# Layer 2's experts on two rows at a time, a channel mix step behind its load, and shorter routing, in a four-layer fp32 forward pass

## The chip, the core and the metric

The kernel runs on one core of a Trainium2 chip. The core has a matmul engine (PE, whose weight loads are listed as PEld), a vector engine (DVE), a scalar engine (ACT), GpSimd (POOL) and SyncE (SP), which here only issues DMA transfers. Every engine works through its own queue in order. All of them read and write the on-chip SBUF; PE writes its results to PSUM. The metric is the device time of the program in microseconds (us), measured on the slowest core, of which there is one.

## What is computed

The input x has 4 rows (the batch) of 512 tokens with 128 features, in fp32. Each of the four layers does the same three things: half a feed-forward block, an attention block, half a feed-forward block, each on a layernorm of x and added to x.

```python
x = x + 0.5 * ffn_i(layernorm(x))
x = x + attn_i(layernorm(x))
x = x + 0.5 * ffn_i(layernorm(x))
```

Layer 0 has a mixture of 8 experts (top 2) and attention with 16 heads of 64; layer 1 a low-rank mixture and a windowed attention; layers 2 and 3 attention with 16 heads of 8, causal in layer 2. The change lies mostly in layer 2's feed-forward block. It is a switch with capacity, row by row:

```python
gates = softmax(tokens @ Wg)                     # 8 experts
expert = argmax(gates)                           # one expert a token
pos = running count of the tokens of that expert in this row
keep = pos < 64                                  # 512 tokens / 8 experts
h = gelu(kept tokens of expert e @ W1[e])        # 128 -> 512
output = gate * (h @ W2[e])                      # 512 -> 128; 0 for tokens not kept
```

Layer 3's feed-forward block is a channel mix: each token is blended with the one before it, by mu and 1 - mu, ahead of its projections.

## The kernel before, in words

Up to about 600 us the program does layer 0's first experts and its attention, and this part is the same in both versions. From there on (line 2636 and below) everything else is one pool of generator "processes": `tile0` to `tile19` (layer 0's second mixture, two blocks of 128 sorted tokens each, `tiled`, L848), `first0` to `first3` (all of layer 1 for one row), and, for n = 0 to 7, which are the four rows ahead of layer 2's attention and the same four behind it, `send{n}`, `take{n}` and `mix{n}`. The attentions of layers 2 and 3 are eight rows k = 0 to 7 (`begin{k}`, then the common processes `turning`, `scoring`, `weighing`, `masking`, `values`, then `turned` and `end{k}`), and layer 3's channel mix is `channels0` to `channels6`.

A process yields requests: an engine (or several that could do the step), a duration, the buffers it needs, and events that it waits for. A loop (`run`, L1413) keeps a clock of its own for each engine, picks the request that can start first, breaks near ties by a rank (`RANK`, L52, a table of tuned numbers), and lets the process issue its instructions. So the order of the instructions on every engine is fixed when the program is built, by these written durations, ranks and surcharges (`DEARER`). On the chip every engine keeps that order, whatever the true durations are.

The steps that the change touches:

- `l2_sent` (L2270, process `send`): layernorm, transposes to features by tokens (L1512), logits (L2283), then the routing on DVE, with an exp on ACT (L2289) in its middle, the running count as two matmuls (L2169, L2170), more DVE, and four indirect DMAs by GpSimd (L2327) that scatter the tokens into slots of a DRAM buffer `row_x`, 64 slots for each expert.
- `l2_taken` (L2335, process `take`): SP loads the row's sorted slots as X (L2345); four transposes (L2351); 32 up matmuls (L2366) with a 128x128 piece of W1 as weights and 64 slots moving; copies out of PSUM; four GELUs on ACT (L2376), which load their function table first; 32 down matmuls (L2384) with 64 columns of hidden units as weights, two side by side in the array; copies; a store to `row_y` (L2393).
- `l2_added` (L2396, process `mix`): four indirect gathers (L2409) and four adds into x (L2415).
- `to_heads` (L2660, process `heads`): once all tiles are done, their pools are released, and SP issues the loads of W2 and of both attentions' and the channel mix's weights, 23 DMAs (L2511). Then `l3_others` (L2418) puts one small DVE step (`nmu` = 1 - mu, L2420) into DVE's order. `heads_at_once` (L1831) writes ones into two V buffers with GpSimd.
- In the heads' attention `scoring` (L1931) and `values` (L1973) are PE's part and the exp (L1947) ACT's. A step covers four heads and one block of 128 keys.

`take{n}` follows `take{n-1}` or `take{n-2}`, `mix{n}` follows `take{n}`, and attention row k begins after `mix{k}` (layer 2) or after the channel mix (layer 3).

Of the kernel before, what the change touches and what calls it, by code (L numbers as in the profile page):

```python
# [11 lines left out]
F32 = mybir.dt.float32  # L12
AF = mybir.ActivationFunctionType
# [4 lines left out]
P = 128  # L18
# [22 lines left out]
def done(b):  # L41
# [9 lines left out]
CLOSE = 0.05  # L51
RANK = {  # L52
    "begin0": 7.13, "begin1": 16.87, "begin2": 2.08, "begin3": -4, "begin4": 2.25, "begin5": 16.3, "begin6": 18.65, "begin7": 5.19,
    "channels0": 2.52, "channels1": 8.5, "channels2": 0.21, "channels3": -14.23, "channels4": 27.64, "channels5": 35.57, "channels6": 55.73,
    "end0": -14.5, "end1": 16.73, "end2": 9.28, "end3": -13.76, "end4": 20.26, "end5": 8.69, "end6": 7.09, "fetching": 36.35, "first0": 12.23,
    "first1": 12.99, "first2": 13.46, "first3": 15.39, "half0": -16.36, "half1": -8.54, "kept0": 9.26, "looked": 68.09, "looked0": 55.15,
    "looked1": 38.53, "looked2": 55.16, "looked3": 44.23, "looked4": 53.01, "looked5": 64.26, "looked6": 56.59, "masking": 45.18, "mix0": 9.64,
    "mix1": 11.51, "mix2": 7.93, "mix3": -7.76, "mix4": 13.42, "mix5": 20.24, "mix6": 9.63, "mix7": 16.21, "placing": -4.73, "scoring": 23.21,
    "send0": -6.03, "send1": 10.23, "send2": 15.94, "send3": 6.71, "send4": 33.89, "send5": 9.79, "send6": 16.23, "send7": 37.79, "take0": -3.51,
    "take1": -6.11, "take2": 22.65, "take3": 5.52, "take4": 16.36, "take5": 23.51, "take6": 10.29, "take7": 21.36, "tile0": 8.75, "tile1": 6.94,  # L60
    "tile2": 4.64, "tile3": 9.21, "tile4": 1.92, "tile5": 9.1, "tile6": -2.3, "tile7": 4.99, "tile8": 9.81, "tile9": 10.06, "tile10": 10.38,
    "tile11": 10.39, "tile12": 11.4, "tile13": 11.41, "tile14": 11.42, "tile15": 10.69, "tile16": 12.44, "tile17": 12.45, "tile18": 12.46,
    "tile19": 12.87, "turning": 58.41, "values": 43.5, "weighing": 38.58, "whole_l2": 4.79, "whole_l3": 12.44,
}
FETCH = 4.0
DEARER = {"PE": 0.0, "ACT": 0, "DVE": 0.3, "POOL": 0.5, "SP": 0.0}
END = object()

def shape_constants():
    c = {}
# [195 lines left out]
def program(ctx: ExitStack, tc: tile.TileContext, a: dict, out: bass.AP, worst):  # L268
# [1562 lines left out]
    def heads_at_once(procs, rows, w, work, w3, late):  # L1831
# [5 lines left out]
        for t in V:  # L1837
            nc.gpsimd.memset(t, 1.0)
# [891 lines left out]
```

## Time and profile before

| | us |
|---|---|
| median of 3 runs (lowest, highest) | 1293.74 (1288.74, 1293.77) |
| the profiled execution's own time | 1290.51 |
| its span, from the first to the last instruction | 1288.7 |
| PE busy | 1158.0 |
| DVE busy | 891.8 |
| ACT busy | 707.1 |
| GpSimd busy | 341.4 |
| mean granted PE clock, share of full speed | 0.958 |

The span is one execution, and the page's durations come from it. PE busy sums intervals whose ends are modelled, since matmuls are pipelined. A row of the groups names line, engine, operation, output and inputs, shapes and count, then busy time, mean of one instruction and the idle time of the engine just ahead of it, with the work that ended it. A row of the timeline begins with start and length in us. Matmuls in fp32 leave two records each, transposes one.

### The profile page before, as it was taken

To read this page: it belongs to the slowest core of one execution; us is meant where nothing else is said; L and a number is where in the kernel's file an instruction comes from. 1 tells how busy PE (TensorE), PEld (TensorE's weight loads), DVE (VectorE), ACT (ScalarE), POOL (GpSimd) and SP (SyncE) were. 2 spreads that over 40 slices of the span, in tenths; PEclk is the share of its full clock that TensorE was granted. 3 is DMA by queue.
4 is the path that set the end of the run, shared out by engine and by line. 5 is a ranking of instruction groups with operands and counts; after the bars stand their busy time and mean duration, and the time that the engine had idled before them with its cause. 6 is when DMAs were issued, how large, how long until landed. Compare 5 with 4: busy or idle time off the path is not lost.

```text
span 1288.7 us, 20383 instructions
## 1 busy us (share of the span) xinstructions
PE 1158.0 (90%) x7066; PEld 614.1 (48%) x7066; DVE 891.8 (69%) x2342; ACT 707.1 (55%) x1030; POOL 341.4 (26%) x323
## 2 busy tenths in 40 slices
PE   5899989999989999997998848798998999999994
PEld 3455544334425335364555426474675665443332
DVE  5697777988988998769668737876637655344233
ACT  2435545654644635442444424466777778778882
POOL 4430223022310400202134535623325233111010
PEclk9899989999999999998999958898999999999998
DMA  8123312111111111101321130001100010000000
GB/s 308 35 72 90 89 57 68 66 60 40 60 62 50 66 50 49 51 1 48 117 66 48 34 109 25 20 16 34 35 25 27 16 34 18 17 25 2 9 9 11
DMA packets 63490, 65.02 MB, mean 50 GB/s; under 512 B 11538, under 2 KB 53907, under 8 KB 62867
## 3 DMA queue, kind: packets, MB, share of 16 engines
q1 hardware_dynamic: 57236, 51.04, 11.8%
q0 software_dynamic: 6144, 12.60, 3.3%
q8 instruction: 59, 0.97, 0.3%
q14 instruction: 51, 0.42, 0.1%
HBM read 29.13 MB, written 17.69 MB: 36 GB/s over the span
## 4 chain that ended last, share of the span: by engine, by line
PE 62%; DVE 18%; issue 8%; DMA 4%; POOL 3%; ACT 3%; SPq 1%; POOLq 0%; DVEq 0%; ACTq 0%
PE big L1931 8%; PE one L1973 7%; PE big L1200 6%; PE one L1214 6%; PE one L2366 4%; PE big L880 3%; PE big L758 3%; PE one L1243 2%; PE one L1522 2%; PE big L603 2%; DMA yg<-sorted_y,ito 2%; DVE sums L1209 2%; PE one L2384 2%; PE big L1150 1%; PE one L1994 1%
## 5 line engine op out<-in xcount | busy, mean ns | idle before, releaser
L1947 ACT ACTIVATE pT<-big 128x1024 f32<-128x1024 f32 (+1 forms) x224 | 205.9, 964 | 43.5 <-PE big L1931 36.7
L1201 ACT ACTIVATE pT<-big 128x1024 f32<-128x1024 f32 x128 | 125.7, 1034 | 54.9 <-PE big L1200 52.8
L1200 PE MATMUL big<-qk 64*128 64x512 f32 x512 | 126.6, 605 | 6.8 <-DVE U L1236 6.8
L1931 PE MATMUL big<-qkq,qkk 32*128 32x512 f32 (+3 forms) x1024 | 127.3, 553 | 1.2 <-ACT pT L1947 1.0
L1214 PE MATMUL one<-pT,V 128*64 128x512 f32 x512 | 116.9, 598 | 0.0
L1973 PE MATMUL one<-pT,V 128*32 128x512 f32 (+3 forms) x1024 | 112.1, 526 | 0.9 <-DVE own L1537 0.6
L583 POOL DMA_INDIRECT sorted_x<-xn,irows x64 | 72.5, 1133 | 69.6 <-DVE share L555 22.4
L1485 POOL TENSOR_TENSOR rs<-rs,root 128x4 f32<-128x4 f32 x35 | 37.4, 1068 | 170.3 <-DVE rs L1483 116.0
L1209 DVE TENSOR_TENSOR sums<-sums,pT 128x1024 f32<-128x1024 f32 x64 | 78.1, 1220 | 5.1 <-ACT qk L1152 0.5
L1200 PEld LDWEIGHTS big<-qk 64*128 64x128 f32 x512 | 46.3, 186 | 69.0 <-issue 40.3
L880 PE MATMUL big<-w_w,xsT 128*128 x156 | 75.3, 614 | 1.8 <-ACT xsT L1352 1.2
L1931 PEld LDWEIGHTS big<-qkq,qkk 32*128 32x128 f32 x1024 | 46.6, 183 | 58.7 <-issue 39.5
L758 PE MATMUL big<-w_w,xsT 128*128 x156 | 73.5, 594 | 0.3 <-issue 0.3
L1291 ACT COPY U<-one 128x512 f32<-128x512 f32 x32 | 18.8, 587 | 94.9 <-PE one L1214 92.8
L839 POOL DMA_INDIRECT yg<-sorted_y,ito x32 | 38.4, 1200 | 122.4 <-DMA sorted_y<-ys 61.5
L1214 PEld LDWEIGHTS one<-pT,V 128*64 128x64 f32 x512 | 33.9, 136 | 77.1 <-issue 72.4
L603 PE MATMUL big<-xnT,w_w 128*128 128x512 f32 x128 | 61.2, 614 | 6.9 <-DVE u L608 5.8
L1959 DVE TENSOR_TENSOR pT<-pT,w_c_tri 128x256 f32<-128x256 f32 (+1 forms) x96 | 48.1, 524 | 21.0 <-ACT pT L1947 20.7
L2366 PEld LDWEIGHTS one<-XT,w_l_w 128*128 128x128 f32 x464 | 54.1, 192 | 12.4 <-ACT hr L1352 4.8
L2366 PE MATMUL one<-XT,w_l_w 128*128 128x64 f32 x464 | 57.2, 276 | 0.7 <-DVE x L350 0.3
L2409 POOL DMA_INDIRECT yg<-row_y,islot x32 | 34.2, 1070 | 75.5 <-DMA row_y<-y 67.9
L605 ACT ACTIVATE t<-big,w_bs 128x512 f32<-128x512 f32 x32 | 21.7, 685 | 56.0 <-PE big L603 33.7
(435 smaller groups left out, 2333.6 us busy)
## 6 DMA issues: line engine op xcount, KB each, us to landing
other<-qk SPq DMA_DIRECT2D x64, 256.0 KB, 2.3
xs<-sorted_x SPq DMA_DIRECT2D x78, 64.0 KB, 1.8
sorted_y<-ys SPq DMA_DIRECT2D x38, 128.0 KB, 1.8
w_w<-in_w SPq DMA_DIRECT2D x2, 2048.0 KB, 13.6
w_l_w<-in_l_w SPq DMA_DIRECT2D x8, 256.0 KB, 3.0
w_l_w<-in_l_w SPq DMA_DIRECT2D x1, 2048.0 KB, 7.7
X<-row_x SPq DMA_DIRECT2D x8, 256.0 KB, 2.8
row_y<-y SPq DMA_DIRECT2D x8, 256.0 KB, 2.3
```

The lines of the kernel that those rows point to most:

```text
L583: apart(nc.gpsimd.indirect_dma_start(out=sorted_x[:, :], out_offset=bass.IndirectOffsetOnAxis(ap=irows[:, b, j, t : t + 1], axis=0), in_=x ...
L603: nc.tensor.matmul(pa[:, m, :], lhsT=w["w13"][:, NE, m, odd, c * P : (c + 1) * P], rhs=xTs[b], start=True, stop=True)
L758: nc.tensor.matmul(pa[:, k, :], lhsT=st[u]["xT"][:, k * P : (k + 1) * P], rhs=w["w13"][:, bass.ds(st[u]["e"][k], 1), m].rearrange("p o a b ...
L880: nc.tensor.matmul(pa[:, k, :], lhsT=xT[:, k * P : (k + 1) * P], rhs=w["w13"][:, bass.ds(e[k], 1), m].rearrange("p o a b -> p (o a b)"), s ...
L1200: nc.tensor.matmul(sT[:, u, :], lhsT=k[r, t * P : (t + 1) * P], rhs=q[r, :], start=True, stop=True)
L1201: nc.scalar.activation(pT[:, :, t % 2, :], sT, AF.Exp, scale=scale)
L1209: nc.vector.tensor_tensor(s, s, pT[:, :, m, :], ALU.add)
L1214: nc.tensor.matmul(po[r, :], lhsT=V[:, t, :], rhs=pT[:, u, t % 2, :], start=(t == 0), stop=(t == NT - 1), tile_position=(0, 64 * u))
L1931: nc.tensor.matmul(sT[j // 2][:, j % 2, c : c + n], lhsT=keys[k][r, t * P : (t + 1) * P], rhs=turns[k, g][r, S - n :], start=True, stop=True)
L1947: nc.scalar.activation(p[:, :, :n], sets[i][h][:, :, :n], AF.Exp, scale=scale)
L1973: nc.tensor.matmul(po[32 * j : 32 * j + 32, S - n :], lhsT=V[k % 2][:, t, NJ * g + j, :], rhs=us[i][j // 2][:, j % 2, c : c + n], start=(t ...
L2366: nc.tensor.matmul(ph[:, j, c, :], lhsT=w["l2_w1"][:, 2 * q + j, c * P : (c + 1) * P], rhs=XT[:, 2 * q + j, :], start=True, stop=True)
```

## The change

1. Layer 2's experts on two rows. `PAIRS = (2, 4, 6)`: rows 0 and 1 keep `l2_taken`; rows 2 and 3, 4 and 5, 6 and 7 go through the new `l2_taken2`, which waits for both sends, loads both rows' X, and lays the transposes side by side, so that an up matmul moves 128 columns (64 slots of each row) against a piece of W1, and a down matmul has 128 columns of hidden units as weights. It stores each row's half of y apart. `mix` of the first row of a pair waits for the common take.
2. The channel mix step `nmu` becomes a process of its own, `others`, that waits for the event `loaded_l3`; `channels0` to `channels3` wait for it. The two memsets of V become processes too (`ones0`, `ones1`).
3. Shorter routing: the gate is 1 / (2 x the sum of exps), so the shares are not formed; the first maximum is found by comparing the logits less their maximum with 0; the exp is off the way to the slots. 21 DVE instructions behind the row's maximum become 18.
4. New durations in many requests, a new rank table, and other surcharges; `turning` no longer offers GpSimd. A helper `kept_warm` is added, whose loop runs over an empty tuple.

The diff, without the rank table and most of the changed durations:

```diff
 }
+PAIRS = (2, 4, 6)
 FETCH = 4.0
-DEARER = {"PE": 0.0, "ACT": 0, "DVE": 0.3, "POOL": 0.5, "SP": 0.0}
+DEARER2 = {"PE": 0.0, "ACT": 0, "DVE": 0.3, "POOL": 0.2, "SP": 0.0}
+DEARER = {"PE": 0.0, "ACT": 0.1, "DVE": 0.3, "POOL": 0.2, "SP": 0.0}
...
+    def kept_warm(t):
+
+        for kind, n, make in () and (("big", 3, big), ("one", 2, one)):
+            a = when(kind, n)
...
                 if t is not None:
-                    e = min(r.ways, key=lambda e: max(t, busy_till[e]) + r.ways[e] + DEARER[e])
+                    dearer = DEARER2 if "begin0" in events else DEARER
+                    e = min(r.ways, key=lambda e: max(t, busy_till[e]) + r.ways[e] + dearer[e])
...
             us = p.req.ways[e]
+            if e == "PE":
+                kept_warm(t)
...
         V = [work.tile([P, NT, H, 32], F32, tag=f"V{m}", name=f"V{m}") for m in range(2)]
-        for t in V:
-            nc.gpsimd.memset(t, 1.0)
         queries, keys, turns, inverse, through = {}, {}, {}, {}, {}
+
+        def ones_in(m):
+            yield POOL(1.9)
+            nc.gpsimd.memset(V[m], 1.0)
+
+        for m in range(2):
+            clock.procs.append(process(f"ones{m}", ones_in(m), 12.0 + 20 * m))
+            clock.procs[-1].ready = clock.done
...
             tokens(pv, xnT, w[layer + "_wv"])
-            yield moving(S, wait=[f"valued{k - 2}"] if k > 1 else [])
+            yield moving(S, wait=[f"valued{k - 2}"] if k > 1 else [f"ones{k}"])
             moved(V[k % 2][:, :, :, :DH].rearrange("p t h d -> p (t h) d"), pv.rearrange("p (n d) -> p n d", d=DH))
...
                 for g in range(NG):
-                    yield any_of({"DVE": 0.46, "ACT": 0.6, "POOL": 0.8}, "qkq", wait=f"q{k}", at=0.0)
+                    yield any_of({"DVE": 0.49, "ACT": 0.72}, "qkq", wait=f"q{k}", at=0.0)
...
 
         return [route(i, b) for i, b in enumerate(rows)], rest()
 
-    def l2_mixed(w, work, b, rooms, key, late):
+    def l2_mixed(w, work, b, rooms, key, late, single):
 
         sent, kept = [], []
-        return l2_sent(w, work, b, rooms, key, sent, kept), l2_taken(w, work, b, rooms, sent, late), l2_added(work, b, rooms, kept, late)
+        take = l2_taken(w, work, b, rooms, sent, late) if single else None
+        return l2_sent(w, work, b, rooms, key, sent, kept), take, l2_added(work, b, rooms, kept, late), sent
 
     def l2_sent(w, work, b, rooms, key, sent, kept):
 
...
+        t0 = clock.done
+        m, order, ex = little([P, NT, NE], "chosen"), little([P, NT, NE], "order"), little([P, NT, NE], "exs")
         gate, best = little([P, NT], "gates"), little([P, NT], "best")
         sofar = little([P, NT - 1, NE], "sofar")
-        yield DVE(1.0)
-        nc.vector.tensor_reduce(sm, sh, AX.X, ALU.add)
-        nc.vector.reciprocal(sm, sm)
-        nc.vector.tensor_tensor(sh, sh, wide(sm, NT), ALU.mult)
-        nc.vector.tensor_reduce(best, sh, AX.X, ALU.max)
-        nc.vector.tensor_scalar(gate, best, 0.5, None, ALU.mult)
-        yield DVE(1.4)
-        nc.vector.tensor_tensor(order, sh, wide(best, NT), ALU.is_equal)
-        nc.vector.tensor_tensor(order, order, w["c_first"].unsqueeze(1).to_broadcast([P, NT, NE]), ALU.mult)
+        yield DVE(1.1)
+        nc.vector.scalar_tensor_tensor(order, sh, 0.0, w["c_first"].unsqueeze(1).to_broadcast([P, NT, NE]), ALU.is_equal, ALU.mult)
         nc.vector.tensor_reduce(best, order, AX.X, ALU.max)
         nc.vector.tensor_tensor(m, order, wide(best, NT), ALU.is_equal)
         nc.vector.tensor_copy(sofar[:, 0, :], m[:, 0, :])
         for t in range(1, NT - 1):
             nc.vector.tensor_tensor(sofar[:, t, :], sofar[:, t - 1, :], m[:, t, :], ALU.add)
-        yield PE(0.5, "psum")
+        t1 = clock.done
+        yield ACT(0.24, at=t0)
+        nc.scalar.activation(ex, sh, AF.Exp)
+        t2 = clock.done
+        yield PE(0.55, "psum", at=t1)
         pp, k = spare()
         before = pp[:, : NT * NE].rearrange("p (t e) -> p t e", t=NT)
         l2_counts(before, m, sofar, w)
+        t3 = clock.done
         islot = little([P, NT], "islot", mybir.dt.int32)
         at, place, slot = little([P, NT, NE], "at"), little([P, NT], "place"), little([P, NT], "slot")
         kept += [gate, islot]
-        yield DVE(1.4)
+        yield DVE(0.85, at=max(t1, t2))
+        nc.vector.tensor_tensor(at, m, w["c_slot0"].unsqueeze(1).to_broadcast([P, NT, NE]), ALU.mult)
+        nc.vector.tensor_reduce(slot, at, AX.X, ALU.add)
+        nc.vector.tensor_reduce(sm, ex, AX.X, ALU.add)
+        nc.vector.tensor_scalar(sm, sm, 2.0, None, ALU.mult)
+        nc.vector.reciprocal(gate, sm)
+        yield DVE(1.15, at=max(clock.done, t3))
         nc.vector.tensor_tensor(order, before, m, ALU.mult)
         free(k)
         nc.vector.tensor_reduce(place, order, AX.X, ALU.add)
-        nc.vector.tensor_tensor(at, m, w["c_slot0"].unsqueeze(1).to_broadcast([P, NT, NE]), ALU.mult)
-        nc.vector.tensor_reduce(slot, at, AX.X, ALU.add)
         nc.vector.tensor_tensor(slot, slot, place, ALU.add)
         nc.vector.tensor_scalar(place, place, float(CAP), float(4 * none), ALU.is_ge, ALU.mult)
         nc.vector.tensor_tensor(slot, slot, place, ALU.add)
...
-            h = work.tile([P, 2, NH, CAP], F32, tag="hr", name="hr", bufs=n * NE // 2)
+            h = work.tile([P, 2, NH, CAP], F32, tag="hr", name="hr", bufs=NE if late else NE // 2)
             moved(h, ph)
             free(k)
             hs.append(h)
         free(kx)
-        yield ACT(2.6 + 2.6)
+        yield ACT(4.8)
         for h in hs:
             nc.scalar.activation(h, h, AF.Gelu_apprx_tanh)
         t0 = clock.done
...
         nc.sync.dma_start(out=ys[:none, :].rearrange("(q p) d -> p q d", p=P), in_=y)
         free(kx, clock.done + 2.5)
+
+    def l2_taken2(w, get, both):
+
+        work = get()
+        NH = HID // P
+        none = NE * CAP
+        X, landed = [], []
+        for rooms, sent in both:
+            yield ask("SP", 0.05, "Xl")
+            took("Xl")
+            X.append(work.tile([P, NT, D], F32, tag="X", name="X", bufs=2))
+            ld = nc.sync.dma_start(out=X[-1], in_=rooms[0][:none, :].rearrange("(q p) d -> p q d", p=P)).ins
+            for k in sent:
+                tc.add_manual_dep(ld, k.name, mybir.DependencyInfo(mybir.DependencyClass.Sync, mybir.DependencyReason.DATA), reason="all tokens' slots")
+            landed.append(clock.done + 5.0)
+        XT = None
+        for i in range(2):
+            yield PE(0.62, "psum", at=landed[i])
+            pt, k = spare()
+            for j in range(4):
+                nc.tensor.transpose(pt[:, j * P : (j + 1) * P], X[i][:, j, :], ident)
+            free("Xl")
+            yield moving(S, *(["wide"] if i == 0 else []))
+            if i == 0:
+                took("wide")
+                XT = work.tile([P, NE, 2, CAP], F32, tag="wide", name="XT", bufs=2)
+            moved(XT[:, :, i, :], pt.rearrange("p (e c) -> p e c", e=NE))
+            free(k)
+        t0 = clock.done
+        hs = []
+        for e in range(NE):
+            yield PE(0.96, "psum", at=t0)
+            ph, k = spare()
+            for c in range(NH):
+                nc.tensor.matmul(ph[:, c * P : (c + 1) * P], lhsT=w["l2_w1"][:, e, c * P : (c + 1) * P], rhs=XT[:, e].rearrange("p i c -> p (i c)"), start=True, stop=True)
+            yield moving(S, "hl")
+            took("hl")
+            h = work.tile([P, NH, P], F32, tag="hr", name="hr", bufs=NE)
+            moved(h.rearrange("p c m -> p (c m)"), ph)
+            free(k)
+            hs.append(h)
+        free("wide")
+        gone, y = [], None
+        for q in range(2):
+            yield ACT(4.8)
+            for h in hs[4 * q : 4 * q + 4]:
+                nc.scalar.activation(h, h, AF.Gelu_apprx_tanh)
+            gone.append(clock.done)
+        for q in range(2):
+            yield PE(3.7, "psum", at=gone[q])
+            py, k = spare()
+            for e in range(4):
+                for c in range(NH):
+                    nc.tensor.matmul(py[:, e * D : (e + 1) * D], lhsT=hs[4 * q + e][:, c, :], rhs=w["l2_w2"][:, 4 * q + e, c, :], start=(c == 0), stop=(c == NH - 1))
+            for _ in range(4):
+                free("hl")
+            yield moving(S, *(["wide"] if q == 0 else []))
+            if q == 0:
+                took("wide")
+                y = work.tile([P, NE, D], F32, tag="wide", name="y", bufs=2)
+            moved(y[:, 4 * q : 4 * q + 4, :].rearrange("p e d -> p (e d)"), py)
+            free(k)
+        for i, (rooms, _) in enumerate(both):
+            nc.sync.dma_start(out=rooms[1][:none, :].rearrange("(e c) d -> c e d", c=CAP), in_=y[CAP * i : CAP * i + CAP])
+        free("wide", clock.done + 2.5)
 
     def l2_added(get, b, rooms, kept, late):
 
...
     qkv = [None] * B
     for kind, n in (("one", 2), ("big", 3), ("xns", 3), ("sT", 4), ("pr", 5), ("pv", 1), ("yb", 5)):
         room(kind, n)
-    for kind, n in (("xn", 3), ("X", 2), ("h", 4), ("yg", 4), ("Xl", 4), ("hl", 8), ("ygl", 4), ("cx", 2), ("t0", 1), ("t1", 1), ("kT3", 1), ("r3", 1)):
+    for kind, n in (("xn", 3), ("X", 2), ("h", 4), ("yg", 4), ("Xl", 2), ("wide", 2), ("hl", 8), ("ygl", 4), ("cx", 2), ("t0", 1), ("t1", 1), ("kT3", 1), ("r3", 1)):
         room(kind, n)
     procs, pools, idle = [], [], [lambda: True]
     rows = [(n, b, causal) for n, causal in (("l2", True), ("l3", False)) for b in range(B)]
...
         yield ask("SP", 0.1)
         right[3].release()
         pools.append(pool("late", side="right"))
+
+    def others(w3):
+        yield DVE(0.2)
+        l3_others(w3, pools[0])
 
     def to_heads():
         yield ask("SP", 0.1)
...
         w2.update(loads(pools[-1], ["l2_w2"], later=behind))
         wa, w3 = heads_weights(pools[-1], behind)
         brought(behind)
-        l3_others(w3, pools[-1])
         events["second"], events["loaded_l2"], events["loaded_l3"] = (clock.done + t for t in (15.0, 22.0, 26.0))
         work = pool("work")
         pools.append(work)
-        yield POOL(3.7)
+        procs.append(process("others", others(w3), 9.0, ["loaded_l3"]))
         idle[0] = heads_at_once(procs, rows, wa, work, w3, late)
         for b in range(B):
-            procs.append(process(f"channels{b}", l3_ffn(b, w3, late, False), 10 + B + b, [f"mix{B + b}", "change"]))
+            procs.append(process(f"channels{b}", l3_ffn(b, w3, late, False), 10 + B + b, [f"mix{B + b}", "change", "others"]))
         for b in range(B - 1):
             procs.append(process(f"channels{B + b}", l3_ffn(b, w3, late, True), 40, [f"end{B + b}"]))
 
...
         clock.done += 4.0
 
     def mixture(n, b, after):
-        first = n < B
-        send, take, add = l2_mixed(w2, (lambda: pools[1]) if first else late, b, row_rooms[b], f"slots{n}", not first)
+        single = n not in PAIRS and n - 1 not in PAIRS
+        send, take, add, sent[n] = l2_mixed(w2, (lambda: pools[1]) if n < B else late, b, row_rooms[b], f"slots{n}", n >= B, single)
         procs.append(process(f"send{n}", send, 10 + n, [after]))
-        k = n - 1 if first else n - 2
-        procs.append(process(f"take{n}", take, 10 + n, [f"send{n}", "fetching", "heads"] + ([f"take{k}"] if k >= 0 else []) + ([] if first else ["change"])))
-        procs.append(process(f"mix{n}", add, 10 + n, [f"take{n}"] + ([f"mix{n - 1}"] if n else [])))
-
-    for b in range(B):
-        mixture(b, b, f"first{b}")
-        mixture(B + b, b, f"end{b}")
+        if single:
+            procs.append(process(f"take{n}", take, 10 + n, [f"send{n}", "fetching", "heads" if n < B else "change"] + ([f"take{n - 1}"] if n else [])))
+        elif n - 1 in PAIRS:
+            pair = [(row_rooms[m % B], sent[m]) for m in (n - 1, n)]
+            procs.append(process(f"take{n}", l2_taken2(w2, late, pair), 10 + n, [f"send{n - 1}", f"send{n}", "fetching", "change"] + ([f"take{n - 2}"] if n > 1 else [])))
+        procs.append(process(f"mix{n}", add, 10 + n, [f"take{n if single or n - 1 in PAIRS else n + 1}"] + ([f"mix{n - 1}"] if n else [])))
+
+    sent = {}
+    for n in range(2 * B):
+        mixture(n, n % B, f"first{n}" if n < B else f"end{n - B}")
 
     units = mix2.tiled(tiles, iwho)
     procs += units
```

## Prediction

> **What bounds the kernel now.** I read the page's sums and slices first, then busy time by stage, then the order of time around the one stage that is not full, and last the groups that the change rewrites.
>
> ```profile
> PE 1158.0 (90%) x7066; PEld 614.1 (48%) x7066; DVE 891.8 (69%) x2342; ACT 707.1 (55%) x1030; POOL 341.4 (26%) x323
> PE   5899989999989999997998848798998999999994
> PEclk9899989999999999998999958898999999999998
> ```
>
> TensorE is busy nine tenths of the span and no other engine seven. One slice, around 750 us, is at 4, and the granted clock falls to 5 with it. By stage (columns: window, length, then busy us and count of PE, PEld, DVE, ACT, POOL, then clock):
>
> ```profile
> 680.00:740.00 60.00, 51.28 (x227) 30.93 (x226) 50.06 (x145) 30.09 (x61) 30.62 (x29) 0.95 0.14 39
> 740.00:775.00 35.00, 17.73 (x52) 11.67 (x52) 13.04 (x64) 8.11 (x21) 13.61 (x13) 0.55 0.33 103
> 775.00:850.00 75.00, 58.93 (x398) 42.92 (x397) 62.97 (x218) 35.30 (x73) 41.53 (x37) 0.89 0.08 24
> 850.00:900.00 50.00, 44.23 (x424) 29.51 (x424) 31.26 (x122) 31.27 (x51) 14.24 (x13) 0.93 0.08 22
> 900.00:1000.00 100.00, 96.14 (x998) 65.07 (x998) 61.54 (x215) 74.94 (x111) 35.83 (x32) 1.00 0.10 29
> 1000.00:1100.00 100.00, 98.49 (x905) 57.34 (x901) 60.27 (x210) 76.76 (x111) 32.50 (x29) 1.00 0.08 24
> 1100.00:1180.00 80.00, 79.88 (x616) 37.17 (x620) 35.18 (x109) 62.62 (x79) 10.93 (x10) 1.00 0.05 14
> ```
>
> From 900 to 1180 us PE is without gaps while ACT, the next, idles a quarter of the time: there a microsecond of matmul taken away is a microsecond of span. From 740 to 900 PE idles 17.3 + 16.1 + 5.8 = 39 us: there the chains bind. The timeline tells the first hole:
>
> ```profile
> ...
> 754.45 0.43 SPq L2511 DMA_DIRECT2D w_l_mu<-in_l_mu  x1
> ...
> 755.87 0.43 SPq L2511 DMA_DIRECT2D w_l3f_wv<-in_l3f_wv  x1
> ...
> 757.42 0.17 DVE L2420 TENSOR_SCALAR nmu<-w_l_mu 128x2 f32<-128x2 f32 x1 [16.77 <-DMA w_l_mu<-in_l_mu]
> ...
> 758.93 2.07 PE L1522 MATMUL one<-w_lora_up,dT 128*128 128x128 f32 x8 [14.71 <-ACT dT L1364]
> ```
>
> At 741.58 us SP began the 23 loads of the heads' weights. VectorE came at once to the small step on l3_mu, the 20th of them, and stood 16.8 us; everything behind it on DVE stood too, and PE idled 14.7 us. What the change rewrites, as groups (busy us, mean ns of one, idle before):
>
> ```profile
> L2366 PE MATMUL one<-XT,w_l_w 128*128 128x64 f32 x464 | 57.2, 276 | 0.7 <-DVE x L350 0.3 <-ACT hr L1352 0.2
> ...
> L2384 PE MATMUL one<-w_l_w,hr 128*64 128x128 f32 x448 | 27.5, 276 | 0.1
> ...
> L2376 ACT ACT_TABLE_LOAD x8 | 10.3, 1283 | 0.1
> ```
>
> and one stretch of the chain in order of time (start, us, what):
>
> ```profile
> 303.52 7.34 PE one L1243 x64
> ```
>
> An up matmul (L2366: 64 columns move against 128x128 weights) costs 57.2/464 = 0.123 us. L1243, in the chain, moves 128 columns with new weights each time at 7.34/64 = 0.115: twice the columns cost no more. A down matmul (L2384, two 64-column tiles side by side) costs 27.5/448 = 0.061. An fp32 matmul leaves two records.
>
> **The change, part by part. A: experts on two rows.** For the six rows 2 to 7, 6 x 64 = 384 up records go, 384 x 0.123 = 47.2 us; 192 of 128 columns come, at 0.115 to 0.123: 22 to 23.6. The 384 down records go, 384 x 0.061 = 23.6; 192 full-width ones come at 0.115: 22.1. Transposes, GELU elements and PSUM copies stay equal (two y copies of 512 per pair instead of four of 256, about 0.3 us). Each row keeps one 256 KB load and one store; the store leaves from 64 partitions instead of 128, nearest row 2.3 us to landing, and two issues follow each other on SP at 0.4. Net -24 to -26 us of PE; I take -24, as part lies in full rows where ACT is nearly level with PE.
>
> **B: the step behind its load.** I expect the hole to stay and only its cause to change. The order of the changed program on SP still has all 23 heads loads ahead of row 0's expert load X. Rows 0 and 1 have now got further before the last tile (tile 16), so row 0's send is over, and on PE the transposes of X stand behind tile 16's last matmuls with only eight matmuls (L1685, 1.9 us) between. In the trace the 23 issues took 741.58 to 756.30, 14.7 us, and X lands a median 2.8 us after its issue; tile's end to first issue was 0.8. So PE waits until 0.8 + 14.7 + 2.8 = 18.3 us after tile 16, less 1.9 of work: 16.4 idle against 14.7 before, **+2**. PE runs in order, so all behind X waits: row 1's output projection, the ups of row 0, rows 2 and 3. The moved step itself costs nothing: DVE comes to it behind a bias step that PE feeds after X, and l3_mu is issued ahead of X. The two V memsets (1.8 us each) now sit in POOL's queue ahead of row 2's gathers; POOL is 13.6 busy of 35 us there; uncovered they would be 3.6.
>
> **C: from the hole to row 0's first scores.** Before, PE resumed at 758.9 and reached L1931 at 837.7. In between it idled 17.6 us more and ran slow:
>
> ```profile
> 770.89 1.92 PE L1558 MATMUL big<-xnT,w_lora_down 128*128 128x512 f32 x2
> ...
> 840.98 1.12 PE L1558 MATMUL one<-xnT,w_lora_down 128*128 128x512 f32 x2
> ...
> 846.48 0.66 PE L2351 MATMUL one<-w_c_ident,X 128*128 128x128 f32 x4 [0.37 <-DVE x L350]
> ...
> 890.00 1.09 PE L2351 MATMUL one<-w_c_ident,X 128*128 128x128 f32 x4 [4.01 <-DMA X<-row_x]
> ```
>
> Such excess over the same instruction later sums to some 9 us. After the change, DVE and POOL have used the hole for rows 2 and 3, and take 0 starts straight after it: transposes and copy 1.3, ups 7.6, GELU with its table load 3.8, downs 4, copy and store 3, four gathers 6.5, norm 5, projections and scores 6: about 37 to 41 us, with about 33 us of PE work inside. I take 8 idle and 5 to 9 slow in place of 26.6: -10 to -14, bounds -16 and 0; I take **-10**.
>
> **D: the wait that pairing adds.** Row 2's experts wait for row 3's send. In the new order row 1's attention ends while take 3's ups run, and nothing but send 5 and take 5's ups is left for PE. Last up to last down: copy 0.7, table load and four GELUs 3.8, then (send 5's exp stands between the GELU groups) two loads, an exp and four GELUs 5.3, then 3.6 of downs: 13.5, with 9.5 of PE work: 4 idle. Last down to row 2's scores: copy 0.7, store and landing 2.7, gathers and add 7, norm 4, projections 4.7: 19 us, with take 5's transposes and ups (8.0) and row 2's own projections (3.6) inside: 7.4 idle. Three restarts like that at 890.00 (1.09 for 0.66, then 1.93 for 1.07 on L1973) lose about 3. Gone is the old wait at that place: 4.0 + 1.9. So 14.4 - 5.9 = **+8**, bounds +3 and +29.
>
> Here the skill speaks against the change. The Trainium skill, "ScalarE: Activation LUTs", section "What ACT_TABLE_LOAD costs", charges about 1.28 us for the load and about 1.38 for a drain, at every switch of function set. Three loads stand in this wait, where before a row needed two. The row has 1283 ns and 0.1 us idle before it, and the GELU began 1.3 us after the load did. By the page the wait would be 3 x 1.38 = 4 us longer, D +12 and the time 1271. I take the row.
>
> **E: shorter routing**: 21 DVE steps after the row maximum become 18, 8 x 3 x about 0.19 = 4.6 us of DVE, and the exp and five steps leave the chain, about 2 us a row. Except in D, where it is counted, PE's other work covers it: 0. **F: durations and ranks** reorder the tile stage (610 to 740 us, PE idle 14.7): 0, bounds -4 and +4. The disabled warm-up helper issues nothing.
>
> Sum: -24 + 2 - 10 + 8 = -24 on the profiled execution's 1290.5 us (span 1288.7 plus 1.8 around it): 1266.5. The shown runs' median is 3.2 us above that execution, so I say **1267**.
>
> **Rivals.** *The hole closes (0.12)*: X is not late, or other work fills it. Then B is -14.7: 1290.5 - 24 - 14.7 - 10 + 8 = 1250. For it: DVE no longer blocks. Against: SP's order. *ACT takes over (0.16)*: a full step needs two exps of 1.02 us, 2.05, and PE's own step near 1213 us was 2.06, so in rows 4 to 7 little is gained; half of A goes, -12, and C gives only 6: 1290.5 - 12 + 2 - 6 + 8 = 1282. Against: ACT idles 22% from 1100 to 1180. *Row 2's wait is bare (0.10)*, the one on the slow side: between take 0's last down matmul (806.5) and row 0's scores (837.7) lie 31.1 us in the trace. PE's order puts take 5's transposes ahead of row 2's; if row 5's X, which needs send 5's scatters, comes late, that cover falls away and D is 31.1 + 4 - 5.9 = +29. With C at 0 and B at +5, for a slow restart: 1290.5 - 24 + 5 + 29 = 1300. It decides once the added waits exceed A's 24. Against: GpSimd and DVE are far less loaded there than around row 0. The forecast keeps 0.62.
>
> **Range.** The forecast's own bounds give 1257 to 1278. Taking in the second rival and half of the first: 1250 to 1287. A measurement of this kernel tells about 0.5%, 6.5 us, from no change. Under 1287: the forecast, the first rival and most of the second, 0.86; within, 0.06; slower, 0.08.
>
> **What would show it.** A: about 192 up and 192 down pair records near 0.115 us each. B: nmu no longer waits, but the transposes of X show a wait of about 16 us on DMA X<-row_x, and the clock drops again. C: first scores some 40 us after that. D: PE gaps of about 4 us before the pair's downs and before take 5's transposes. E: no new DVE wait. I am wrong if the PE hole is gone, if full rows run at ACT's pace, or if row 2 idles over 25 us.

## The result, and the profile after

The changed kernel takes 1287.57 us in the median of 20 runs (1280.65 to 1300.24), the kernel before 1293.49 (20 runs, 1288.3 to 1296.8). The ratio is 0.9957, 95% interval 0.9941 to 0.9973: some 6 us faster, a small gain but clear of noise, where 27 were forecast (24 by the forecast's own sum, which starts from an execution 3.0 us below this median). The first profiled execution took 1300.24 us, at the top of those runs and at a lower clock, so the lines below are from a second trace of the same kernel, which took 1286.38 us with a span of 1284.5.

The page's sums and slices of the changed kernel:

```profile
PE 1151.6 (90%) x6682; PEld 605.5 (47%) x6682; DVE 894.3 (70%) x2328; ACT 700.4 (55%) x1015; POOL 328.3 (26%) x320
...
PE   5899989999999999998899947889979999999993
...
PEclk9899989999999999989899978799979999999997
```

384 matmul records have gone, and PE's busy time has fallen by only 6 us. The slice at 4 is still there, and there are new thin slices at 7 around 785 us and at 7 around 950 us, with a lower granted clock beside them. By stage, in the columns used before:

```profile
740.00:775.00 35.00, 16.71 (x83) 13.52 (x82) 15.78 (x50) 7.84 (x21) 16.43 (x17) 0.71 0.40 122
775.00:850.00 75.00, 60.52 (x394) 45.55 (x397) 53.69 (x200) 40.20 (x79) 35.99 (x35) 0.86 0.07 21
850.00:900.00 50.00, 46.03 (x437) 27.77 (x429) 43.14 (x142) 32.71 (x52) 20.57 (x18) 0.97 0.07 22
900.00:1000.00 100.00, 90.17 (x776) 64.31 (x774) 55.82 (x201) 66.73 (x101) 36.55 (x35) 0.93 0.13 38
1000.00:1100.00 100.00, 97.31 (x809) 47.20 (x808) 58.99 (x195) 76.69 (x108) 15.90 (x15) 1.00 0.04 12
1100.00:1180.00 80.00, 77.48 (x549) 35.52 (x547) 43.80 (x142) 64.72 (x82) 17.28 (x16) 1.00 0.06 18
```

From 740 to 900 PE idles 36.7 us against 39.1 before. From 900 to 1180, which was full, it now idles 15.0 us against 5.5, and the clock is no longer 1 everywhere. The first hole, from the timeline (start, length, what, and in brackets the idle time before it):

```profile
754.48 3.61 PE L1704 MATMUL one<-w_c_ident,pv 128*128 128x128 f32 x16 [2.72 <-DVE pv L1697]
...
767.02 0.43 SPq L2603 DMA_DIRECT2D w_l3f_wv<-in_l3f_wv  x1
767.69 0.38 SPq L2372 DMA_DIRECT2D X<-row_x  x1
...
770.48 1.09 PE L2378 MATMUL one<-w_c_ident,X 128*128 128x128 f32 x4 [12.39 <-DMA X<-row_x]
...
774.53 0.99 POOL L975 DMA_INDIRECT yg<-sorted_y,ito  x1 [11.01 <-DVE st L1497]
```

SP issues row 0's X right behind the last of the 23 weight loads, and PE stands for it: 12.4 us, besides 2.7 that it waited for DVE ahead of L1704. The 23 issues take 14.8 us, of which 3.7 are one pause behind the eighth (3.9 in the kernel before), whose cause is open. GpSimd stands 11.0 us, because DVE, whose next steps need PE, stands too. The pairs, as groups:

```profile
L2475 PE MATMUL one<-w_l_w,hr 128*128 128x128 f32 x192 | 23.9, 286 | 0.0
L2456 PE MATMUL one<-XT,w_l_w 128*128 128x128 f32 x120 | 18.3, 303 | 0.8 <-ACT XT L1355 0.7
...
L2456 PE MATMUL big<-XT,w_l_w 128*128 128x128 f32 x72 | 10.2, 297 | 0.0
```

192 records each, at 23.9/192 = 0.124 and 28.5/192 = 0.148 us; some of the ups run at half clock. And the wait that the pair of rows 2 and 3 adds:

```profile
939.23 8.71 PE L2475 MATMUL one<-w_l_w,hr 128*128 128x128 f32 x64
...
948.59 1.38 SPq L2485 DMA_DIRECT2D row_y<-y  x2
950.20 1.50 SPq L2433 DMA_DIRECT2D X<-row_x  x2
...
953.91 1.94 PE L2442 MATMUL one<-w_c_ident,X 128*128 128x128 f32 x8 [5.97 <-DMA X<-row_x]
...
967.05 1.07 PE L1910 MATMUL one<-xnT,w_l_wks 128*128 128x512 f32 x2
```

Row 2's projections come 967.05 - 947.94 = 19.1 us after the end of the pair's last down matmul (939.23 + 8.71). PE has take 5 and row 2's own transposes in between, and take 5's X comes late, behind send 5's scatters and the two stores.

### The profile page after: what moved, and what is told of

It reads as the page before. It is cut to its first block, busy times and chain, and to the rows that moved or that the text cites. A ratio compares the mean times of both kernels' runs of the same rounds, so it can differ in the third digit from the quotient of the medians.

```text
span 1298.4 us, 19615 instructions
## 1 busy us (share of the span) xinstructions
PE 1162.9 (90%) x6682; PEld 614.5 (47%) x6682; DVE 895.4 (69%) x2328; ACT 700.7 (54%) x1015; POOL 327.5 (25%) x320
## 3 DMA queue, kind: packets, MB, share of 16 engines
q1 hardware_dynamic: 57236, 51.04, 11.8%
## 4 chain that ended last, share of the span: by engine, by line
PE 65%; DVE 20%; issue 5%; DMA 4%; ACT 3%; POOL 2%; SPq 1%; DVEq 0%; POOLq 0%; ACTq 0%
PE big L1956 8%; PE one L1998 7%; PE big L1203 6%; PE one L1217 6%; PE big L761 4%; PE big L606 3%; PE one L1541 3%; PE one L1246 2%; PE big L883 2%; PE one L2475 2%; DVE sums L1212 2%; PE big L1153 2%; PE one L2456 1%; PE big L635 1%; PE one L2019 1%
## 5 line engine op out<-in xcount | busy, mean ns | idle before, releaser
L1956 PE MATMUL big<-qkq,qkk 32*128 32x512 f32 (+3 forms) x1024 | 132.0, 560 | 1.3 <-ACT qkq L1367 0.6
L1504 POOL TENSOR_TENSOR rs<-rs,root 128x4 f32<-128x4 f32 x35 | 37.1, 1059 | 234.4 <-DVE rs L1502 188.2
L1956 PEld LDWEIGHTS big<-qkq,qkk 32*128 32x128 f32 x1024 | 49.4, 185 | 63.5 <-issue 41.3
L353 DVE TENSOR_TENSOR x<-x,one 128x512 f32<-128x512 f32 x31 | 21.2, 684 | 57.3 <-PE one L1541 32.5
L1984 DVE TENSOR_TENSOR pT<-pT,w_c_tri 128x256 f32<-128x256 f32 (+1 forms) x96 | 52.4, 562 | 3.3 <-ACT pT L1972 3.0
L322 POOL TENSOR_TENSOR rs<-rs,root 128x4 f32<-128x4 f32 x16 | 20.7, 1298 | 118.5 <-DVE rs L321 118.4
L1998 PEld LDWEIGHTS one<-pT,V 128*32 128x32 f32 x1024 | 24.2, 108 | 55.8 <-issue 38.6
```

What stands on the lines that cost most here:

```text
L1956: nc.tensor.matmul(sT[j // 2][:, j % 2, c : c + n], lhsT=keys[k][r, t * P : (t + 1) * P], rhs=turns[k, g][r, S - n :], start=True, stop=True)
L1984: nc.vector.tensor_tensor(d, d, w["c_tri"].unsqueeze(1).unsqueeze(1).to_broadcast([P, 2, len(parts), P]), ALU.min)
L1998: nc.tensor.matmul(po[32 * j : 32 * j + 32, S - n :], lhsT=V[k % 2][:, t, NJ * g + j, :], rhs=us[i][j // 2][:, j % 2, c : c + n], start=(t ...
```

## The experiments

To set kernels with unequal work beside each other, each kind of matmul was given its mean full-clock time over six traces, and the work still to come was summed at several times. The lead is how much less a kernel has still to do than the kernel before at the same time. The columns are after_again, no_pairs, nmu_only, x_first and b_nmu_routing, one execution each, and another way of counting a matmul's time moves an entry by up to 2 us:

| us | changed | no pairs | step alone | X load first | step and routing |
|---|---|---|---|---|---|
| 577 | 17.9 | -3.2 | -0.9 | 19.2 | -0.9 |
| 740 | 24.4 | 2.5 | 0.6 | 24.9 | 0.3 |
| 780 | 29.6 | 8.3 | 11.5 | 34.3 | 11.6 |
| 900 | 26.9 | 6.7 | 16.4 | 37.1 | 14.8 |
| 980 | 13.8 | 3.0 | 14.4 | 23.6 | 12.8 |
| 1060 | 11.8 | 1.2 | 16.3 | 21.5 | 6.3 |
| 1180 | 6.6 | -3.7 | 15.7 | 15.7 | 0.3 |

The kernels with pairs have 22.7 us less to do from the start (1129.7 against 1107.0 in all), so their 17.9 at 577 us is 4.8 lost, not won. More on that stands at the end of the account of the prediction.

**A second trace of the changed kernel** (after_again), nothing edited.

> The changed kernel, nothing edited, for a second trace. Theory: the time lies at 1283 to 1290 us, PE idles 10 to 16 us at the transposes of row 0's X, and the granted clock stays below 0.8 from about 760 to 800 us, longer than the 740 to 775 us of before. Rival (the low clock until 820 us in the first trace was chance): the clock is back at 1.0 by 785 us, and the lost gain shows as idle PE near row 2 instead.

1286.38 us; PE idled 2.7 and 12.4 us at the hole. Of 755 to 775 us the clock was 0.59 on average and of 790 to 810 us 0.76. The theory holds for the idle time, not for the clock, which was back at 1 from 774.8 to 785.0. The low clock came in pieces, and idle PE shows near row 2 as well, as the rival had it: the loss has more than one place.

**X ahead of the weights** (x_first). SP issues row 0's X before the 23 loads, which now wait for the event that `l2_taken` sets behind X's load; no other instruction changes its place.

```diff
+        happened(f"asked_{b}")
...
-        brought(behind)
...
+        procs.append(process("weights", weights(behind, clock.done), 0, ["asked_0"]))
```

> The changed kernel with one transfer moved: SP issues row 0's load of X ahead of the heads' 23 weight loads; every other order is the same. Theory (the loads on SP make the hole, and the low clock after it follows from the hole): the 12 us wait for X falls to under 3, the clock stays near 1 from 755 to 800 us, and the time falls by 12 to 22 us, to about 1268 to 1274. Rival (what stands behind X is bound by the weights' landing anyway): the wait moves to the down matmuls or to row 0's projections, and the time falls by less than 6.

1278.11 us, ratio 0.9875 (0.9842 to 0.9907), 9.5 below the changed kernel:

```profile
753.64 0.36 SPq L2372 DMA_DIRECT2D X<-row_x  x1
...
756.63 0.60 PE L2379 MATMUL one<-w_c_ident,X 128*128 128x128 f32 x4
```

The transposes follow with no wait. It is the idle time that was won: 27.8 us from 740 to 900 against 36.7. What half clock cost there stayed at 14.8 us against 14.7 (PE's busy time in low-clock stretches, halved), so the part of the theory that counted on the clock fell.

**No pairs** (no_pairs): `PAIRS = ()`, with the kernel before's counts of buffers for single rows; all else kept.

> The changed kernel with every row of layer 2's experts by itself, all else kept. Theory (pairs take 15 to 20 us of matmul away and cost 8 at row 2): 7 to 14 us slower than the changed kernel, 1294 to 1301. Rival (row 2's wait eats all that pairs save): within 3 us of the changed kernel or faster, and PE's gap near row 2 is gone.

1296.66 us, ratio 1.0026 (1.0012 to 1.0040). The pairs are worth 9.1 us, as the theory said. In the traces PE's full-clock work differs by 21.2 us, idle time by 4.7 and half clock by 7.4 the other way (21.2 - 4.7 - 7.4 = 9.1). Idle time and half clock together differ by as much between 900 and 980 us alone, here in after_again and then in no_pairs:

```profile
900.00:980.00 80.00, 70.30 (x603) 55.21 (x602) 44.20 (x166) 52.47 (x81) 26.78 (x26) 0.91 0.12 34
...
900.00:980.00 80.00, 76.87 (x784) 52.08 (x780) 49.30 (x182) 56.40 (x84) 26.62 (x25) 1.00 0.10 30
```

It also means that everything in the change except the pairs makes the kernel 3 us slower.

**Pairs alone** (pairs_only): the kernel before with `l2_taken2`, its `mixture` and its buffers; old routing, channel mix step, durations and ranks.

> The kernel before with the pairs alone; its routing, its channel mix step, its durations and its ranks are kept. Theory (the pairs carry the gain, the rest of the change moves little): 6 to 14 us faster than before, 1280 to 1288. Rival (the new ranks and durations are needed to hide row 2's wait): not faster than before, with PE gaps of over 15 us ahead of row 2's scores.

1321.19 us, ratio 1.0230 (1.0199 to 1.0261): 28 us slower. The rival holds, though the 16.0 us that PE idles from 940 to 980 are several waits, the longest 8.0 (on ACT). The clock is at half for 20.5 us there, and PE idles 4 to 5.5 us in each of three later stretches of 20 us. The same pairs gain 9 us in the new order and cost 28 in the old one.

**The channel mix step alone** (nmu_only, and again as b_nmu_only): the kernel before, `nmu` as a process that waits for `loaded_l3`. In the trace one DVE instruction stands elsewhere, and every other order is as it was.

> The kernel before with one DVE step moved: nmu waits for its load as a step of its own and stands later in DVE's order; every other order is the same. Theory (the step is what holds DVE and, through it, PE; PE has layer 1's rows 2 and 3 ready there and needs no X): the 14.7 us gap falls to under 4 and the time falls by 9 to 14 us, to 1280 to 1285. Rival (another step is held by the same loads, so that the gap only changes its cause, as the prediction said of the changed kernel): the gap stays over 10 us and the time falls by less than 3.

1279.57 us, ratio 0.9888 (0.9862 to 0.9914): 14 us from one small instruction, more than twice what the whole change brings. The stage of the hole, to be set beside the one before (PE 17.73 busy, clock 0.55):

```profile
740.00:775.00 35.00, 25.50 (x109) 18.79 (x109) 24.65 (x101) 10.60 (x28) 22.33 (x22) 0.73 0.39 123
```

In the old order PE has layer 1's rows 2 and 3 ready at that point, and the lead of some 16 stays up to 1180 us.

> The kernel before with the channel mix step moved. Theory (the 14 us gap closes, on any chip): 0.985 to 0.992 of before, and 5 to 10 us faster than the changed kernel of this call.

1279.30 us, 0.9888 (0.9863 to 0.9914), 8.7 below the changed kernel beside it.

**The step put back in the changed kernel** (nmu_back, b_nmu_back). Other instructions change their places with it: the orders of PE, DVE, ACT and GpSimd differ from some 800 us on.

> The changed kernel with the channel mix step put back behind the loads as before, where DVE comes to it at once. Theory (in the changed order the step is masked: PE stands at row 0's X, which comes behind the same loads): within 4 us of the changed kernel, 1284 to 1292, nmu waits over 10 us on DVE and PE still idles about 12 at X. Rival (the step is worth the same 14 us in both orders): 9 to 14 us slower, 1297 to 1302.

It ran on a chip that takes 1319.68 us for the kernel before, and without the changed kernel beside it; 1304.83 us, 0.9884 (0.9850 to 0.9917), says little by itself. Beside the changed kernel:

> The changed kernel, as the base of this call. Theory (its ratio to before depends on the chip only through the clock): 0.985 to 0.997 of before.

> The changed kernel with the channel mix step put back behind the loads. Theory (masked by the wait for X; in the earlier trace PE idled 20 us there in one gap, against 15 in two): 0 to 5 us slower than the changed kernel of this call. Rival (worth the same in both orders): 9 to 14 us slower.

b_after 1287.99 us, 0.9957 (0.9940 to 0.9974); b_nmu_back 1291.38 us, 0.9990 (0.9974 to 1.0006). The step, with the order that it brings, is worth 3.4 us in the new order and 14 in the old one. Its trace shows two waits on top of each other:

```profile
768.52 0.17 DVE L2512 TENSOR_SCALAR nmu<-w_l_mu 128x2 f32<-128x2 f32 x1 [16.59 <-DMA w_l_mu<-in_l_mu]
...
771.65 3.54 PE L1704 MATMUL one<-w_c_ident,pv 128*128 128x128 f32 x16 [19.93 <-DVE pv L1697]
775.03 0.60 PE L2378 MATMUL one<-w_c_ident,X 128*128 128x128 f32 x4
```

By the time that PE has done what DVE held back, X has landed, and its transposes don't wait; when DVE is not held, PE stands for X. Each hides the other.

**The routing on top of the step** (nmu_routing, b_nmu_routing): `l2_sent` of the changed kernel in nmu_only, old ranks.

> The kernel before with the channel mix step moved and with the shorter routing; the old ranks and the old durations elsewhere. Theory (routing is covered by PE's other work): within 4 us of the kernel with the step alone, 1276 to 1284. Rival (the shorter chain from the logits to the slots lets rows start earlier): 5 us faster or more.

1311.42 us on the chip at 1319.68, 0.9941 (0.9918 to 0.9963), without nmu_only beside it. Beside b_nmu_only:

> The same with the shorter routing. Theory as it stood (routing is covered): within 4 us of the step alone. Rival (the routing's new requests change the order of everything after them, and the old ranks, which were set for the old routing, do not fit): 5 to 12 us slower than the step alone, as its ratio of 0.994 against 0.989 hints.

1296.14 us, 1.0027 (1.0010 to 1.0044): 16.8 us slower than the step alone. The rival holds. The lead equals that of the step alone within some 2 us up to 1020 us (13.9 against 16.2), then falls by 7.6 in 40 us, and row 5's projections start at 1079.4 us where they started at 1066.6 with the step alone. The stage with the step alone and with the routing on top, and the place in the timeline:

```profile
1020.00:1060.00 40.00, 40.00 (x377) 22.96 (x377) 26.10 (x85) 31.04 (x45) 13.62 (x12) 1.00 0.09 27
...
1020.00:1060.00 40.00, 36.11 (x329) 23.06 (x326) 17.11 (x49) 24.27 (x36) 9.00 (x8) 0.87 0.09 26
...
1038.81 0.88 ACT L1498 ACTIVATE cx<-x,off,rs 128x128 f32<-128x128 f32 x2 [4.14 <-DVE off L1487]
...
1040.20 0.66 PE L1512 MATMUL one<-w_c_ident,cx 128*128 128x128 f32 x4 [2.15 <-ACT hr L1352]
```

In ACT's order a norm for the channel mix stands ahead of a copy out of PSUM and the next exp, and waits 4.1 us for DVE; PE waits for ACT, and the clock is at half for 10.2 us from 1041.5 on. Up to 1180 us the lead falls by another 6.0, with 3.6 us of idle PE where the step alone has 0.1. So it is the order that came out of the new requests that costs here, and not the three DVE steps less; that is read from the trace, as no run has the new steps in the old order.

**Rows 2 and 3 by themselves, rows 4 to 7 in pairs** (pairs_46), and the same with X first (x_pairs_46): `PAIRS = (4, 6)`.

> The changed kernel with rows 2 and 3 each by itself and rows 4 to 7 in pairs. Theory (row 2's wait for row 3 costs 12 us in the trace and saves 7 of matmul there): no gap over 4 us and no low clock from 920 to 975 us, and 3 to 7 us faster than the changed kernel, 1281 to 1285. Rival (the wait is only moved to row 4's pair, or the single rows' own chains wait as long): within 2 us of the changed kernel or slower.

> Row 0's X load ahead of the weights' loads, and rows 2 and 3 each by itself. Theory (the two losses are independent): the two gains add, 9 plus 3 to 7 us below the changed kernel, 1271 to 1276. Rival (the two share slack): no faster than the kernel with the X load moved alone, 1278.

1299.82 us, 1.0051 (1.0029 to 1.0073), and 1287.01 us, 0.9934 (0.9908 to 0.9960). Both theories fell. The stretch at row 2 is near full (75.2 of 80 us from 900 to 980), but the wait turns up at row 4's pair, where no other rows are left:

```profile
1020.00:1060.00 40.00, 29.91 (x238) 14.98 (x239) 29.05 (x98) 18.54 (x28) 18.21 (x16) 0.90 0.15 40
```

The changed kernel has 38.52 busy there. A likely reason, not shown: while rows 2 and 3 stand in the changed kernel, take 5 and rows 4 and 5 get ahead, so that the wait is partly paid back later. X first brings 12.8 us here, near its 9.5: that gain does add.

**One stretch of GELUs for a pair** (x_gelu): X first, and the eight GELUs of a pair in one request, so that a pair loads GELU's table once.

> Row 0's X load ahead of the weights' loads, and the eight GELUs of a pair in one go, so that a pair loads the GELU's table once and not twice. Theory (in the trace of the last pair PE idles 2.5 us while ACT does load, GELUs, load, one exp, load, GELUs, load; the first pair has a like row): 1 to 4 us faster than with the X load moved alone, 1274 to 1277. Rival (one long stretch of GELUs holds back the exps as much): within 1 us, or slower.

1276.32 us, 0.9862 (0.9837 to 0.9887): 1.8 below x_first, with intervals that overlap; not told apart. It has the lowest median of the study.

**The hole filled** (hole_filled, b_hole_filled): 40 matmuls on PE, whose result is overwritten, ahead of the transposes of row 0's X.

```diff
+        for _ in range(40 if sent and not late and b == 0 else 0):
+            nc.tensor.matmul(pt[:, :P], lhsT=ident, rhs=ident, start=True, stop=True)
```

> The changed kernel with 40 matmuls added on PE whose result nobody reads, just ahead of the transposes of row 0's X, where PE idles 12 us; they take about 9 us at full clock and all other orders are the same. Theory (the low clock after 760 us follows from the idle PE): the low clock after the hole shrinks from 14 us or more to under 7, and the time falls by 2 to 6 us, to 1281 to 1286, with less spread. Rival (the low clock follows from the whole thin stretch from 740 to 830 us): low clock and time stay as they are, within 2 us.

1301.53 us on the chip at 1319.68, 0.9856 (0.9827 to 0.9884), without the changed kernel beside it. On a chip that takes 1293.23 us for the kernel before:

> The changed kernel with 40 unread matmuls where PE idles ahead of row 0's X. Theory (the idle stretch brings the low clock that follows it): the low clock between 755 and 785 us falls from 14 us to 7 or less, the time by 2 to 6 us against the changed kernel, that is 0.991 to 0.994 of before if before takes about 1293. Rival (the low clock belongs to the thin stretch as a whole): 0.995 to 0.998.

1284.39 us, 0.9920 (0.9895 to 0.9945), 3.6 below b_after (0.9957, 0.9940 to 0.9974; the intervals just touch).

```profile
757.34 9.10 PE L2378 MATMUL one<-w_c_ident 128*128 128x128 f32 x80
770.69 1.11 PE L2380 MATMUL one<-w_c_ident,X 128*128 128x128 f32 x4 [4.26 <-DMA X<-row_x]
```

From 755 to 775 us the clock is 0.86 instead of 0.61, and the 13.7 us of half clock in the hole are 3.4. So of the time lost at the hole some 4 us belong to the clock; the size is rough, since b_after ran on another chip of the same speed.

**X first without pairs** (x_no_pairs).

> Row 0's X load ahead of the weights' loads, and all rows by themselves. Theory (the wait for X and the pairs are independent): 9 to 10 us below the changed kernel without pairs, 1286 to 1289; so the new ranks and durations without pairs are 6 to 10 us slower than the old ones with the channel mix step moved (1279.6). Rival (they share slack): over 1291.

1307.13 us on the chip at 1319.68, 0.9915 (0.9876 to 0.9955). Kernels that ran on both chips have ratios that are 0.006 to 0.011 lower on that one, so that this would be 0.998 to 1.002 on a chip that takes 1293, an estimate of 1291 to 1296 us. In the trace the clock is at half for 17.1 us between 900 and 940 us, which takes back 7.9 us of what was won at X. That speaks for shared slack, but the low clock can also be this chip's, and it isn't settled.

## Why the prediction was wrong, step by step

**A held.** -24 was taken; the PE work of the kernel fell by some 22 us at full clock. Against no_pairs, ups fall by 21.4 and downs by 1.0.

**B held**, cause and size: PE stands at X behind SP's 23 loads, 15.1 us of idle against 14.7, where +2 was said (12.4 of it at X, where one wait of 16 was forecast).

**C held in its own stage.** From the end of the hole to row 0's first scores there are 47.6 us instead of 78.8 (37 to 41 were said), with 9.2 idle and 9.4 of half clock, together 12.3 less than before. But the reason given was wrong: DVE and POOL did little for rows 2 and 3 in the hole, they stood in it (DVE 17.7 us, POOL 11.0). And the sum took the rows of layer 1 that were put off as free: from there to 900 us the losses are 12.6 against 8.9, where row 2's old wait of 5.9 was booked as gone.

**D held as a wait.** 14.4 was its gross size; from 900 to 980 us idle and half clock are 15.3 us in the changed kernel and 3.1 without pairs, 12.2 more. So A and D together, -24 + 14.4 = -9.6, are what the pairs measure alone: -9.1. The agreement holds for this order only, since in the old one the same pairs cost 28, and the places differ: 4 us of idle were forecast ahead of the pair's downs, where PE has no wait, and most of it is the 6.0 us for take 5's X and the low clock, 13.7 us that cost 5.6.

**E and F are the step that failed**: "PE's other work covers it: 0" and "reorder the tile stage (610 to 740 us, PE idle 14.7): 0, bounds -4 and +4". All that isn't pairs was put at +2 - 10 - 5.9 + 0 = -13.9 us, and measures +3.2 (no_pairs): 17.1 us off, out of a miss of 20.6. Of the rest, 3.0 are the base, since the sum started from an execution 3.0 us below the median. The bound looked at one stage, while durations, ranks and the routing's new requests set the order on all five queues up to the end. Measured apart, the step alone gives -14, and the routing on top +16.8 with the old ranks; the new ranks and durations without the routing were not run. With the new ranks and durations the kernel without pairs is where that one is (1296.7 and 1296.1), and now X's wait, 9.5, is part of it. Then its lead falls from 6.7 at 900 us to -3.7 at 1180: PE idles 11.2 us there against 5.5, in some twenty waits of 0.2 to 1.7 us on DVE and ACT, none of them a place of its own. What makes up the remaining 5 us of that fall is open. With pairs the fall from 980 to 1180 is 7.2; at the last pair ACT goes load, GELUs, load, one exp, load, GELUs, load, and PE idles 2.5, each time until DVE.

The rival that ACT takes over had the better time (1282), but not for its reason: from 980 to 1180 us ACT is busy 155.7 of 200 us, and of PE's nine waits six are on DVE, 4.4 us of 5.0. None of the prediction's three signs of being wrong came true: the hole is there, full rows aren't at ACT's pace, and row 2 idles less than 25 us. The prediction also missed what lay in the trace before. The 14.7 us gap could be closed by that one step in the old order, and the changed order gives that up by putting X where the step had stood.

4.8 us of the loss lie ahead of 577 us, where the order on PE, DVE, ACT and GpSimd is the same in all these kernels (on all four it is the same up to 638 us of the trace of before). For no_pairs it is 3.2, so of the 17.1 some 14 are left for what lies behind. The same instruction (L693, later L696) starts at 601.7 in the trace of before and at 602.5 and 605.2 in two traces of nmu_only, at 601.8 in b_nmu_routing, and at 605.1 to 609.5 in those with the new ranks (on chips where before takes 1293). Half-clock stretches of 3.4 us come or stay away there: up to 575 us the clock is at half for 20.5 us in the trace of before and for 27.3 in the changed kernel's. Whether the change has a part in it isn't settled.

## What to carry to other kernels

Where an order is fixed by written durations and ranks, an edit is costed twice: its own instructions, and the order that it gives everything behind it. The second can be as large as the first, and only a run of each part alone tells them apart. When one wait goes, ask which instruction stands next in that queue and what it waits for: here one DVE step was worth 14 us in one order and 3 in the other, where more than the step moved. And a pair saves what its rows cost only if other rows' work lies in its wait; moving the pairs moved the wait with them.

## What the runs showed of the hardware

The granted clock is 0.5 or 1, and in the traces' records of it the low stretches last multiples of 3.4 us (the last one of a trace aside). In the changed kernel the one in the hole begins 3 us after PE stops and ends 4 us after it resumes. The Trainium skill, "TensorE: Matmul & The Clock Gate", Part 1, puts the gate's window at 3413 ns and says that it runs by itself; the steps agree. By that page one busy window brings full clock back. After a later gap, of 4.2 us up to 802.5, the clock stayed at half for 10.2 us, three steps of 3.4, in which PE was busy for 0.63, 0.80 and 1.00 of the time; behind the wait at 952 it was 0.51, 0.80 and 1.00. So there a step with gaps did not bring the clock back and a full one did, which agrees with the page; ahead of 560 us two low stretches went on for a step more. The clock also fell without an idle step: at 785.0, 826.0, 873.7 and 938.6 us it fell behind steps in which PE was busy for 0.51, 0.50, 0.84 and 0.41. So a stretch with many small gaps costs clock, too. In the hole, 9.1 us of unread matmuls in 12.4 us of idle time brought about 3.6 us.

GELU's table load took 1283 ns in all traces, pairs or not, with 0.1 us of idle in all ahead of a trace's five to eight loads, and GELU began 1.29 us after its load did. The row of the changed kernel's pairs:

```profile
L2468 ACT ACT_TABLE_LOAD x5 | 6.4, 1283 | 0.1
```

So the 1.38 us drain that the prediction weighed never showed, and it was right to take the row.
